# A two-layer convolution block on one core: one xs store a unit, a third place for layer 0's outputs, moved expert and weight steps, Newton square roots

## The chip, the core and the metric

The kernel runs on one core of one Trainium2 chip. The metric is the device time of an execution in microseconds; several executions are made and their median is given. Engines are named as in the profile: PE (matrix multiply), DVE (vector), ACT (scalar, activation), POOL (GpSimd), SP (issues most of the transfers; "SPq" and "ACTq" are the queues of SP and ACT).

## The reference, cut to what matters

The input x has shape (4, 64, 256, 256), float32. Two blocks are added to it in turn, each on a GroupNorm of 32 groups (two channels a group):

```python
x = x + L0(_gn(x))
x = x + L1(_gn(x))

def L0(x):                                   # layer 0
    h = _gelu(_conv2d(x, c1_w, ((1, 1), (1, 1))))          # 3x3, 64 -> 64
    xa, k = jnp.split(_c1x1(h, c2_w, c2_b), 2, axis=1)
    xs = _conv2d(xa, sh_w, ((0, 0), (1, 1)), groups=C) + sh_b   # 1x3, per channel
    xs = _conv2d(xs, sv_w, ((1, 1), (0, 0)), groups=C) + sv_b   # 3x1, per channel
    xs = _gelu(xs)
    weights = softmax(xs.mean(axis=(2, 3)) @ gate_w.T)     # top 2 of 3 kept, in mask
    out = xs
    for i, (w1, b1, w2, b2, w3, b3) in enumerate(experts): # ranks 2, 4, 8
        e = _c1x1(_c1x1(k, w2, b2) * _c1x1(xs, w1, b1), w3, b3)
        out = out + e * mask[:, i][:, None, None, None]
    return _c1x1(out, proj_w, proj_b)

def L1(x):                                   # layer 1
    h = relu(batchnorm(conv3x3(x, quantize(w1), b1)))      # statistics over all images
    h = batchnorm(conv3x3(h, quantize(w2), b2))
    return relu(h + x)
```

## The kernel before, in words

Layer 0 is cut into 64 **units**, 16 an image, each of 16 image rows (8 on each half of the 128 partitions). A unit's 3x3 convolution is made by a transform over rows: POOL forms differences of input rows in a single buffer `v` (`x_fourths`, `x_seconds`, `v_inner`, `v_outer`); PE multiplies them with `us`, the weights scaled by the image's GroupNorm (`front_conv`, tiles `ps_c`, products 1 to 4 first and the outer products 0 and 5 later); DVE puts the products together in PSUM (`butterfly_a` to `butterfly_d`, L631 to L650); ACT takes the GELU (`front_h`, L658). The outer products add onto the bank that `butterfly_c` has just written (L643, L644). The two separable convolutions follow for each half of a unit: PE multiplies the vertical taps (`front_taps_a` and `front_taps_b`, tile `ps_a`, one PSUM place named "a"), ACT and DVE add the horizontal ones (`front_taps_i`, L699; `front_taps_h`, L706 to L717, the last to read the place), and ACT takes the GELU into xs (`front_xs`, L730), whose row sums feed the gate. Between the two tap groups a tick (`divide`, L506, a one-column memset) separates matmuls on the bank; it runs on DVE for the first image and on POOL from slot 16 on.

For every two units PE makes the low-rank parts of the experts: `front_k` (tile `ps_k`, 32 matmuls, from h) in even slots, `front_q` (tile `ps_q`, 16 matmuls, from xs) in odd ones; DVE multiplies the two (`front_low`, L771). xs goes to DRAM with one transfer for each half of a unit, issued by ACT (`xs_store`, L735), the low ranks through SP (`low_store`).

An image's gate needs the mean over all its xs, so its **output** runs an image later: four slots after the image's end, chunk k of the 16 is loaded again (`xs_load` L844, `low_load` L854, and x itself into y, `out_load` L835), PE multiplies with the gated weights (`out_open`, tile `ps_o`), DVE adds onto y (`out_add`, L880) and takes its statistics (L885), SP stores y (`out_store`, L893). The y tiles have the tag "o" with two places. At the same time the GroupNorm statistics of a later image are taken from further loads (`stats_load` L410; `stats_group` on DVE L415, `stats_piece` on ACT L448).

Layer 1 runs over the same images in chunks of 16 rows: `conv1_load` (`yn`), differences on POOL (L343), a split of each operand in an upper and a lower part on ACT and DVE (L346, L353), 128x128 matmuls (L296, tiles `ps_hm` and `ps_h`), and an exit on DVE (`leave`, L318) into h, which ACT squares (L382) and stores (L998). h lies in a place "h1", or, for odd chunks of later images and for odd chunks after the second of the first, in the place "x" that layer 0's loads used (`conv1_out`). Its BatchNorm needs all images; then conv2 runs the same way, and a last pass adds and stores.

**Order of the work.** It is written out by hand. `at(step, order, call)` puts a call in a plan; a unit's slot is two steps, and `at_slot(u, pos, ...)` puts positions below 6 in its first step and 6 to 12 in its second. `plan_front`, `plan_stats`, `plan_out`, `plan_out_late` and `plan_conv1` fill the plan, which is sorted and issued; each engine then runs its own instructions in exactly that order, and a wait of one holds all behind it on that engine. Slots 64 to 66 have no unit of their own, and the table `TAIL` spreads what is left of them over layer 1's steps. "Slot u" below is the time from unit u's first L631 to the next unit's. The order of a slot on PE, which the change touches, is this:

```python
at_slot(u, 2, front_taps_a, u - 2, 1)
at_slot(u, 4, front_taps_b, u - 2, 1)
at_slot(u, 5, front_conv, u, (0, 5))
at_slot(u, 7, front_taps_a, u - 1, 0)
at_slot(u, 8, front_k, ...)   # front_q in odd slots
at_slot(u, 9, front_taps_b, u - 1, 0)
```

**Roots and weights.** `combine` makes a GroupNorm's mean and 1/std out of partial moments: two tiny matmuls with one-column steps between, the square root on ACT (L282), a reciprocal on DVE (L284). It is a generator, advanced at places that the plan names (`stats_end` for the inputs, `out_end` for the outputs). `weights1` quantizes layer 1's two weight sets in three steps each (DVE, L249 to L261), at slots 7 to 12.

Of the kernel before, what the change touches and what calls it, by code (L numbers as in the profile page):

```python
# [11 lines left out]
BF16 = mybir.dt.bfloat16  # L12
AF = mybir.ActivationFunctionType
# [6 lines left out]
P = 128  # L20
# [21 lines left out]
def conv_preact_kernel(ctx: ExitStack, tc: tile.TileContext, io, col128, colset, col64):  # L42
# [82 lines left out]
    eps_bn = const.tile([P, 1], F32, name="eps_bn")  # L125
    nc.vector.memset(eps_bn, BN_EPS)
# [13 lines left out]
    outer = lconst.tile([P, 2, W], F32, name="outer")  # L140
# [33 lines left out]
    def weights():  # L174

        m64_t = work.tile([P, 2, GF], F32, tag="xs", name="m64", bufs=4)
# [22 lines left out]
        for i in range(2):  # L199
            o = outer[:, i, :]  # L200
            nc.vector.tensor_scalar(o, zeros[:, 0:W], sh_bias, None, ALU.add)
            nc.vector.tensor_tensor(o[:, 0 : W : W - 1], o[:, 0 : W : W - 1], end, ALU.subtract)
            nc.vector.tensor_scalar(o, o, c128("sv")[:, 2 * i : 2 * i + 1], None, ALU.mult)
# [41 lines left out]
    def weights1(name):  # L245
# [5 lines left out]
        nc.vector.reciprocal(inv, scale)  # L251
        yield
        nc.vector.tensor_scalar(w, w, inv, ROUND, ALU.mult, ALU.add)
        nc.vector.tensor_scalar(w, w, ROUND, None, ALU.subtract)
        nc.vector.tensor_scalar(w, w, QMAX, -QMAX, ALU.min, ALU.max)
# [7 lines left out]
    def combine(mv, n, avg, eps_t, out, name, engine=nc.vector):  # L263
# [16 lines left out]
        nc.vector.tensor_reduce(var, ps[:, 0:n], AX.X, ALU.add)  # L280
        yield
# [4 lines left out]
    def group_norm(st, avg, out, name, engine):  # L286
        mv = stat.tile([P, 1, 2], F32, tag="mv", name=f"mv_{name}")
        nc.vector.bn_aggr(mv[:, 0, :], flat(st))
        yield
        yield from combine(mv, 1, avg, eps, out, name, engine)  # L290
# [183 lines left out]
    def stats_end(b):  # L474
# [10 lines left out]
        yield from combine(mv, n, c128("avg4"), eps, own, f"x{b}", nc.vector if b == 0 else nc.gpsimd)  # L485
# [215 lines left out]
    def front_taps_h(u, sub):  # L701
# [19 lines left out]
        for at_n, i, row in ((0, 0, 0), (NOCT - 1, 1, 2 * GP - 1)):  # L721
            if n == at_n:
                rows = slice(i * C, i * C + C)
                nc.vector.tensor_tensor(t[rows, row, :], t[rows, row, :], outer[rows, i, :], ALU.subtract)

    def front_xs(u, sub):
        b, k = divmod(u, NCH)
        n = 2 * k + sub
        x = xss[b, n] = work.tile([P, 2, GF], F32, tag="xs", name=f"xs_{b}_{n}", bufs=4)
        nc.scalar.activation(flat(x), flat(open_t.pop((u, sub))), AF.Gelu, accum_out=pooled[b][:, n : n + 1])  # L730

    def xs_store(u, sub):
        b, k = divmod(u, NCH)
        n = 2 * k + sub
        nc.scalar.dma_start(xs_d[b][:, n, :], flat(xss[b, n]))  # L735
# [24 lines left out]
    def front_q(b, j):  # L760
# [874 lines left out]
```

## Time and profile before

| | |
|---|---|
| Median of three executions | 2964.82 us (2963.71 to 2973.92) |
| The profiled execution | 2959.65 us, span 2957.8 us |
| Busy over the span | PE 79%, DVE 83%, ACT 68%, POOL 57% |
| Transfers | 915.35 MB in 135715 packets, 309 GB/s mean |

Times inside the span are counted from its start. The stages, with the limits that the slots and the layers give:

| Stage | from us | to us | length us |
|---|---|---|---|
| Statistics of image 0, slots 0 and 1 | 0 | 98.0 | 98.0 |
| Slots 2 to 11, image 0, no output yet | 98.0 | 278.0 | 180.0 |
| Slots 12 to 19 | 278.0 | 422.9 | 144.9 |
| Slots 20 to 24, output of image 0 begins | 422.9 | 516.2 | 93.3 |
| Slots 25 to 43 | 516.2 | 899.0 | 382.8 |
| Slots 44 to 62 | 899.0 | 1258.5 | 359.5 |
| Start of layer 1 | 1258.5 | 1331.5 | 73.0 |
| Rest of conv1 | 1331.5 | 1923.0 | 591.5 |
| conv2 | 1923.0 | 2514.0 | 591.0 |
| Last pass | 2514.0 | 2957.8 | 443.8 |

How to read the views. A table of stretches gives the busy microseconds of each engine in each stretch (with the number of instructions), the granted clock of PE as a share, the mean busy share of the 16 DMA engines, and GB/s. A chain of waits is followed back from the last instruction of a window, each time to what released it: start, length, engine and what it did; "issue" is time without a wait that the trace shows. A row of waits names who waited for whom, with the sum in us, the count and the longest. Names like `ps_a` or `y` are tiles; "a<-b" is written from b.

### The profile page before, as it was taken

Reading aid. Unit: us, or ns where it says so; the run is one execution under the profiler, and the core shown is the slowest. Engines: PE = TensorE matmul, PEld = TensorE weight load, DVE = VectorE, ACT = ScalarE, POOL = GpSimd, SP = SyncE. Lnnn points to the kernel's source line nnn. Section 1 sums busy time; section 2 is a strip of 40 time slices with the busy share of each in tenths; the row PEclk is TensorE's granted clock in tenths of the full one; section 3 lists DMA queues with packets and bytes.
Section 4 is the critical chain, followed back from the end, with each engine's and each line's share of the span. In section 5 each row is a group of like instructions: output and inputs, shape, how many; then the busy total and the mean of one; then the engine's idle time right before and its main releaser. Section 6 shows DMA issues by size and latency. Waiting matters only on the chain.

```text
span 2957.8 us, 52737 instructions
## 1 busy us (share of the span) xinstructions
PE 2345.4 (79%) x21576; PEld 1502.1 (51%) x21576; DVE 2448.4 (83%) x2811; ACT 2007.1 (68%) x2183; POOL 1676.8 (57%) x1252
## 2 busy tenths in 40 slices
PE   2888899999999999979999999989999999000000
PEld 1444445444445555546666667867788888000000
DVE  6688678888888988869999999979999898976664
ACT  4777888787776665567676667978888887432221
POOL 6988888787778888733545546735555555000000
PEclk9999999999999999999999999999999999555555
DMA  8665579999999999859999997747777764999999
GB/s 352 233 239 209 199 269 369 354 351 350 355 349 320 320 319 327 290 203 320 343 367 361 332 360 272 270 176 274 258 267 264 270 219 156 375 412 423 420 424 409
DMA packets 135715, 915.35 MB, mean 309 GB/s; under 512 B 14960, under 2 KB 15728, under 8 KB 40880
## 3 DMA queue, kind: packets, MB, share of 16 engines
q1 hardware_dynamic: 107824, 777.74, 71.1%
q10 hardware_dynamic: 27648, 134.23, 11.3%
q8 instruction: 170, 2.79, 0.4%
q14 instruction: 73, 0.60, 0.1%
HBM read 573.74 MB, written 338.17 MB: 308 GB/s over the span
## 4 chain that ended last, share of the span: by engine, by line
PE 50%; DMA 29%; DVE 13%; ACT 3%; POOL 2%; issue 2%; SPq 0%; ACTq 0%; DVEq 0%; POOLq 0%
PE ps_h L296 18%; PE ps_c L513 9%; DMA y<-in_xp 7%; PE ps_a L513 7%; PE ps_h2m L296 6%; DMA y_end<-y_d 5%; DMA y_d<-y 4%; DMA out<-h 4%; DMA h<-h_d 4%; PE ps_o L513 4%; DMA yn<-y_d 3%; PE ps_hm L296 3%; DVE t L714 2%; DVE t L717 2%; PE ps_k L744 1%
## 5 line engine op out<-in xcount | busy, mean ns | idle before, releaser
L296 PE MATMUL ps_h<-diff,w_q 128*128 128x512 f32 x3072 | 755.2, 400 | 12.4 <-DVE h L318 11.9
L296 PEld LDWEIGHTS ps_h<-diff,w_q 128*128 128x128 f32 x3072 | 577.0, 189 | 190.6 <-issue 20.4
L513 PE MATMUL ps_c<-v,us 64*64 64x256 f32 x9216 | 534.0, 380 | 28.6 <-DVE ps_c L644 25.4
L343 POOL TENSOR_TENSOR d<-yn 128x1024 f32<-128x1024 f32 x128 | 348.9, 2745 | 299.3 <-DMA yn<-y_d 164.8
L513 PEld LDWEIGHTS ps_c<-v,us 64*64 64x64 f32 x9216 | 360.7, 134 | 174.4 <-issue 17.6
L343 POOL TENSOR_TENSOR d<-h 128x1024 f32<-128x1024 f32 x126 | 307.1, 2459 | 206.4 <-DVE diff L351 143.6
L513 PE MATMUL ps_a<-h,av 64*64 64x512 f32 x4080 | 386.5, 492 | 47.3 <-DVE t L717 40.1
L318 DVE SCALAR_TENSOR_TENSOR h<-ps_h,scale_w,m 128x1024 f32<-128x1024 f32 x256 | 323.1, 1279 | 78.7 <-PE ps_h L296 56.3
L561 POOL TENSOR_TENSOR x<-x 128x512 f32<-128x512 f32 x256 | 328.8, 1284 | 12.7
L1497 ACT ACTIVATE h<-h,shift,gn 128x2048 f32<-128x2048 f32 (+1 forms) x65 | 134.3, 2067 | 276.0 <-DVE h L1496 273.8
L513 PEld LDWEIGHTS ps_a<-h,av 64*64 64x64 f32 x4080 | 153.7, 133 | 322.2 <-issue 212.8
L382 ACT ACTIVATE junk<-h,less_h 128x2048 bf16<-128x2048 f32 (+3 forms) x134 | 256.2, 1912 | 13.6 <-DVE h L318 13.5
L1496 DVE SCALAR_TENSOR_TENSOR h<-h,inverse,y_end 128x2048 f32<-128x2048 f32 (+1 forms) x65 | 150.5, 2317 | 122.0 <-DMA y_end<-y_d 122.0
L699 ACT ACTIVATE t<-ps_a,tap_bias,m 128x1016 f32<-128x1016 f32 x128 | 153.3, 1197 | 117.0 <-PE ps_a L513 91.4
L880 DVE SCALAR_TENSOR_TENSOR y<-ps_o,ob,y 128x1024 f32<-128x1024 f32 x128 | 164.0, 1281 | 50.9 <-PE ps_o L513 26.6
L730 ACT ACTIVATE xs<-t 128x1024 f32<-128x1024 f32 x128 | 134.8, 1053 | 103.8 <-DVE t L717 90.2
L353 DVE SCALAR_TENSOR_TENSOR diff<-d,gn,diff 128x1024 fp32r<-128x1024 f32 x128 | 202.0, 1608 | 0.9 <-ACT diff L346 0.5
L296 PE MATMUL ps_h2m<-odd,w_q 128*128 128x512 f32 x768 | 193.5, 401 | 5.9 <-ACT odd L359 3.8
L296 PE MATMUL ps_hm<-odd,w_q 128*128 128x512 f32 x768 | 194.0, 402 | 2.8 <-DVE t L717 1.3
L346 ACT ACTIVATE diff<-d 128x1024 fp32r<-128x1024 f32 x128 | 135.3, 1057 | 81.1 <-POOL d L343 79.5
L553 POOL TENSOR_TENSOR x<-x,x 128x512 f32<-128x512 f32 x128 | 160.5, 1275 | 34.2 <-ACT x L547 34.2
L717 DVE SCALAR_TENSOR_TENSOR t<-ps_a,m,t 128x1020 f32<-128x1020 f32 x128 | 163.9, 1280 | 4.6
(256 smaller groups left out, 4235.2 us busy)
## 6 DMA issues: line engine op xcount, KB each, us to landing
x<-in_xc SPq DMA_DIRECT2D x64, 1280.0 KB
h<-h_d SPq DMA_DIRECT2D x64, 1152.0 KB
yn<-y_d SPq DMA_DIRECT2D x60, 1152.0 KB
xs_in<-in_xp SPq DMA_DIRECT2D x64, 1024.0 KB
xs_d<-xs ACTq DMA_DIRECT2D x128, 512.0 KB
xs_in<-xs_d SPq DMA_DIRECT2D x64, 1024.0 KB
y<-in_xp SPq DMA_DIRECT2D x64, 1024.0 KB
y_d<-y SPq DMA_DIRECT2D x64, 1024.0 KB
```

What stands on the lines that cost most here:

```text
L296: nc.tensor.matmul(ps, wq[w][:, kind, kx, :], t[:, rows, kx : kx + W], start=(j == 0), stop=(j == len(terms) - 1))
L318: nc.vector.scalar_tensor_tensor(h.rearrange("p (e k) w -> p e (k w)", e=2), ps.rearrange("p e k w -> p e (k w)"), w_scale[w], m.unsqueeze ...
L343: engine.tensor_tensor(raw.rearrange("p (g r) w -> p g r w", g=2), *pair, ALU.subtract)
L353: nc.vector.scalar_tensor_tensor(lower, raw, scale, upper.bitcast(F32), ALU.mult, ALU.subtract)
L382: nc.scalar.activation(junk[rows, 0:n], flat(h), AF.Square, bias=less[name][rows], accum_out=total)
L513: last[:] = [nc.tensor.matmul(ps[o, at_out[0] : at_out[1], :], w[i], rhs[i], **flags)]
L553: nc.gpsimd.tensor_tensor(x4[:, j - 1], x_rows(u, j + 2), x4[:, j - 1], ALU.subtract)
L561: nc.gpsimd.tensor_tensor(x[:, r : r + 2], x[:, r + 2 : r + 4], x[:, r : r + 2], ALU.subtract)
L699: nc.scalar.activation(t[:, :, inside], ps[:, :, inside], AF.Identity, bias=tap_bias, scale=sh[:, 1:2])
L717: nc.vector.scalar_tensor_tensor(t[:, :, 0 : W - 1], ps[:, :, 1:W], sh[:, 2:3], t[:, :, 0 : W - 1], ALU.mult, ALU.add)
L880: nc.vector.scalar_tensor_tensor(y, ps.rearrange("p x s w -> p x (s w)"), out_bias[b], y, ALU.add, ALU.add)
L1496: nc.vector.scalar_tensor_tensor(at_h, at_h, inverse[:, b : b + 1], y[:, a:e, :], ALU.mult, ALU.add)
```

## The change

Layer 0's xs gets one tile for both halves of a unit (two of them, where there were four half tiles), stored with one transfer at the place of the second half's. The y tiles get a third place in layer 0's own pool for every third chunk. In slots up to 19, `front_k` stands at position 4.5 instead of 8, and so does `front_q` for three of its four half units, with the fourth left at 8. The DVE statistics at position 4.1 go to 6.125 in slots below 16. `weights1` has four steps, at slots 5 to 8 and 9, 10, 11 and 14. The square roots of the GroupNorms other than the first go to three Newton steps on POOL from a bit estimate on DVE; BatchNorm's stay on ACT. In layer 1, h of chunk 1 of image 0 lies in the place "x", the row differences of both halves share a tile, the second splits of chunk 1 stand behind the taps, and y of the late outputs is stored a step later. `outer` keeps one row a partition, and the second epsilon column goes.

The diff, cut:

```diff
+    HALF = 0.5
+    MAGIC = 1597463007.0
+    def root(var, n, y, name):
+        nc.vector.tensor_scalar(var, var, 1.0 / n, eps, ALU.mult, ALU.add)
+        nc.vector.tensor_scalar(y.bitcast(I32), var.bitcast(I32), -HALF, MAGIC, ALU.mult, ALU.add)
+        t = stat.tile([P, 1], F32, tag="ct", name=f"root_{name}")
+        for _ in range(3):
+            yield
+            nc.gpsimd.tensor_scalar(t, var, y, y, ALU.mult, ALU.mult)
+            nc.gpsimd.tensor_scalar(t, t, -HALF, 1.0 + HALF, ALU.mult, ALU.add)
+            nc.gpsimd.tensor_tensor(y, y, t, ALU.mult)
...
         nc.vector.tensor_reduce(var, ps[:, 0:n], AX.X, ALU.add)
+        if step:
+            yield from root(var, n, out[:, 1:2], name)
+            return
...
     def front_xs(u, sub):
-        x = xss[b, n] = work.tile([P, 2, GF], F32, tag="xs", name=f"xs_{b}_{n}", bufs=4)
-        nc.scalar.activation(flat(x), flat(open_t.pop((u, sub))), AF.Gelu, accum_out=pooled[b][:, n : n + 1])
+        if sub == 0:
+            xss[u] = work.tile([P, 2, 2, GF], F32, tag="xs", name=f"xs_{u}", bufs=2)
+        x = xss[u][:, sub].rearrange("p s f -> p (s f)")
+        nc.scalar.activation(x, flat(open_t.pop((u, sub))), AF.Gelu, accum_out=pooled[b][:, n : n + 1])
-    def xs_store(u, sub):
-        nc.scalar.dma_start(xs_d[b][:, n, :], flat(xss[b, n]))
+    def xs_store(u):
+        nc.scalar.dma_start(xs_d[b][:, 2 * k : 2 * k + 2, :].rearrange("p a b -> p (a b)"), x)
...
     def out_load(b, k):
-        ys[b, k] = chunk_out(f"y_{b}_{k}", "o", 2)
+        if k % 3 == 2 and (b < B - 2 or b == B - 2 and k < 11):
+            ys[b, k] = front_pool.tile([P, CPAIR, W], F32, tag="third", name=f"y_{b}_{k}")
+        else:
+            ys[b, k] = chunk_out(f"y_{b}_{k}", "o", 2)
...
     def conv1_out(b, k, g):
-            if k % 2 and (b > 0 or k > 2):
+            if k % 2:
...
-                at_slot(u, 6.135, xs_store, u - 2, 1)
+                at_slot(u, 6.135, xs_store, u - 2)
-                at_slot(u + 1, 1.6, xs_store, u - 1, 0)
+            alone = u < NCH + 4
-                at_slot(u, 8, front_k, *divmod(j, NOCT // 4))
+                at_slot(u, 4.5 if alone else 8, front_k, *divmod(j, NOCT // 4))
-                at_slot(u, 8, front_q, *divmod(j, NOCT // 4))
+                if alone:
+                    at_slot(u, 4.5, front_q, *divmod(j, NOCT // 4), range(3))
+                at_slot(u, 8, front_q, *divmod(j, NOCT // 4), range(3 if alone else 0, 4))
...
-            for n in range(3):
-                at_slot(7 + 3 * i + n, 7.3, next, chain, None)
+            for u in ((5, 6, 7, 8), (9, 10, 11, 14))[i]:
+                at_slot(u, 7.3, next, chain, None)
...
-                at_slot(int(s), 4.1 if s - int(s) < 0.5 else 7.25, stats_group, b, *group)
+                early = 6.125 if int(s) < NCH else 4.1
+                at_slot(int(s), early if s - int(s) < 0.5 else 7.25, stats_group, b, *group)
...
-                at(step + 1, 13.3, out_store, b, n // 2)
+                at(step + 2, 13.3, out_store, b, n // 2)
...
-            at(*late(up0, 13.12), conv1_upper, b, k, 0)
-            at(*late(up1, 13.14), conv1_upper, b, k, 1)
+            behind = b == 0 and k == 1
+            at(*late(up0, 13.36 if behind else 13.12), conv1_upper, b, k, 0)
+            at(*late(up1, 13.37 if behind else 13.14), conv1_upper, b, k, 1)
-            at(*((t, 1.3) if first else late(low0, 13.22)), conv1_lower, b, k, 0)
+            at(*((t, 1.3) if first else late(low0, 13.45 if behind else 13.22)), conv1_lower, b, k, 0)
```

## The prediction

> **What bounds the kernel now.** I cut the span into stages, with slot borders at the starts of L631 (the first butterfly instruction, one a slot), and read the busy time of each engine in each.[...]
>
> ```profile
> 98.00:203.60 105.60, 93.00 (x1381) 50.80 (x1375) 82.17 (x124) 84.04 (x117) 92.41 (x73) 1.00 0.67 232
> 203.60:278.00 74.40, 63.99 (x952) 34.62 (x944) 63.00 (x93) 53.20 (x72) 64.69 (x50) 1.00 0.56 200
> ...
> 422.90:516.20 93.30, 93.16 (x1336) 48.19 (x1329) 81.55 (x104) 76.32 (x108) 76.68 (x71) 1.00 1.00 372
> 516.20:899.00 382.80, 359.42 (x5033) 183.70 (x5028) 317.69 (x414) 299.27 (x420) 298.16 (x296) 1.00 0.96 350
> 899.00:1258.50 359.50, 358.79 (x5060) 185.79 (x5056) 317.57 (x410) 217.55 (x268) 293.78 (x295) 1.00 0.91 315
> 1258.50:1331.50 73.00, 53.78 (x382) 30.61 (x371) 47.23 (x55) 43.22 (x48) 26.84 (x17) 0.94 0.55 204
> ```
>
> The columns: stretch, length, busy us of PE, weight loads, DVE, ACT, POOL, granted clock, DMA share, GB/s. Slots 44 to 62 (899 to 1258.5) are PE without a gap, and so are slots 20 to 24. Time above PE's busy time is lost in three places: slots 2 to 19, slots 25 to 43 (23.4 us), and the start of layer 1 (19.2 us). I asked each for its chain of waits. In slots 2 to 19 no engine is full:
>
> ```profile
> 154.80 0.69 DVE ps_c L644
> 155.49 1.19 DVE st_x L415 x2
> 156.68 0.14 DVE t L706
> 156.82 0.02 issue
> 156.85 1.29 DVE t L714
> 158.14 0.02 issue
> 158.16 1.29 DVE t L717
> 159.45 0.14 issue
> 159.59 2.38 PE ps_a L513 x24
> 161.97 1.85 PE ps_q L766 x16
> 163.82 0.59 PE ps_a L513 x8
> 164.42 5.24 PE ps_c L513 x94
> ```
>
> Two statistics instructions stand ahead of the taps, whose last instruction (L717) frees the one "a" bank; only then does PE go on, and k or q stand in the rest of its path. In slots 25 to 43:
>
> ```profile
> 589.49 13.76 DMA y_d<-y
> ...
> 603.33 20.72 DMA y<-in_xp
> 624.05 0.04 DVEq L880
> ```
>
> A store of y frees a place, the load into it lands, the next sum and store follow at 629.40: 39.9 us for two slots, since there are two places. That is the stage's pace: 382.8/19 = 20.15 a slot against PE's 18.92. At the start of layer 1:
>
> ```profile
> DVE h L318 <- DMA h_d<-h: 12.5, 1, 12.5
> PE ps_h L296 <- DVE h L318: 8.6, 1, 8.6
> ```
>
> Chunks 1 and 2 of h share the one "h1" place; chunk 2 waits for chunk 1's store, and PE behind it.
>
> **k and q of image 0, and the statistics (slots 2 to 19).** Nothing is added: k's 32 matmuls, and 12 of q's 16, move ahead of the outer products. In slot 6 of the timeline PE stood 0.23 us for the tick, 0.77 for L644 ahead of the outer products and 0.72 for L717 (1.13 in slot 7). With 1.9 us of k or q put into the 0.77, and 1.2 us of statistics behind the taps, L717 is through before PE needs the bank: 17.38 - 0.77 - 0.72 and 17.76 - 0.77 - 1.13, plus 0.23 in each for a tick now uncovered behind the taps, gives 16.1 a slot. ACT, behind a statistics piece and k's copy, reaches its first copy up to 0.8 us later than PE would, so I take 16.3. The moved statistics now stand ahead of DVE's second tick; with the butterfly before them they are 2.7 us beside a tap group of 2.38 on PE, which itself starts later, so they hide, or cost 0.3. Slots 2 to 7: 105.6 to 98.2, -7.4. Bounds: 15.5 (PE's 93.00/6), and 17.6, no gain, should POOL (92.41/6 = 15.4, ahead of its waits) set the pace.
>
> Slots 8 to 11 lose more: slots 8 and 11 took 19.29 and 20.50, each with three weight instructions in a row (1.18 + 1.52 + 1.05 us) ahead of the taps. The change lays one to a slot; at most the copies (2.1 us) stand together. I take 16.6 a slot with what spills over: 74.4 to 66.4, -8.0. Slots 12 to 15 took 73.4 with PE at 63.5 and ACT at 63.4: 68.1, -5.3. In 16 to 19 the tick is POOL's, in order behind the row differences. k used to stand between the two tap groups and hid that tick; moved, it pushes the outer products and the POOL work waiting on them by about as much as it saves. I take 0, bounds -4 and +4. Together -21.
>
> **Newton steps.** Seven of eight GroupNorm roots leave ACT. L282's table loads read 1283 ns; the square root itself 0.29 us, and the gelu table comes back: 2 x 1.28 + 0.29 = 2.9 us of ACT each. The Trainium skill ("ScalarE: Activation LUTs", What ACT_TABLE_LOAD costs) adds a drain of about 1.38 us per switch, so 5.6; the group's idle time ahead of its seven loads here is 0.1 us in all, so I use 2.9. It is worth something only in slot 14 (ACT 17.9 of 19.29, counted above); elsewhere ACT has 3 us of slack a slot. Added: two DVE instructions near 0.2 for a reciprocal, and nine POOL ones per root near 0.19 (the gate's L814) with their issue, 2.4 us in three places, behind which row differences queue. POOL has 3 us of slack a slot where PE is full. In layer 1 DVE's last product waits for POOL's third step, with its lower differences (L353) and exits (L318) queued behind: before it waited for ACT's root, so -1 to +4 in all; I take +1.
>
> **Third place for y (slots 25 to 43).** The loop of 39.9 us now spans three slots, 13.3 each: gone. Next late is PE at 359.4 us, or the transfers: the stage moved 134.17 MB. Here a rule speaks against the change. The Trainium skill ("DMA: Bandwidth & Descriptors", Where 436 GB/s comes from) has HBM bind a core at about 358 GB/s. By it the stage can't be under 134.17/0.358 = 374.8 us, a gain of 8. But slots 20 to 24, the same streams before the loop binds, ran 372 GB/s with PE full, and the end reaches 424 in the page's last slices. The row decides: 134.17/0.370 = 362.6, -20. Bounds -8 and -23.4 (PE).
>
> **One xs store a unit.** 64 transfers of 1 MB for 128 of half: ACT issues 64 fewer (0.33 us of its queue each, beside its work), and the same bytes move. By the trace's packets 4 KB on ACT's queue take 159 ns at the median, 8 KB in layer 1 309: 2.8% of a seventh of the traffic, under 0.1 us a slot, which the 370 leaves out. Some ACT issues also wait for a y store (six ACT waits, 17.6 us); those go with SP's lag. The new wait is in the rivals.
>
> **Start of layer 1.** h of chunk 1 goes to the x place, so chunk 2 needs chunk 0's store, issued at 1303.91; with the same 11.4 us it lands at 1315, before ACT's m is through at 1319.8. DVE then starts near 1319.9 instead of 1330.17, and PE, done with its last group at 1322.95, loses its 8.57 us. Chunk 1's differences now stand behind the taps; PE waited 3.35 us at 1281 for L717, behind a L353 that waited for ACT: -2. If k's buffer or POOL's differences (wait of 12.6 for q) are late instead, half is left. -10, bounds -5 and -13.
>
> The stores of y one step later in layer 1 and the smaller edge tile pass nothing on SP's queue that a wait depends on, and the weights' first tile is loaded once: 0.
>
> **Sum.** -21 - 20 - 10 + 1 = -50: 2909.6 on the profiled execution, 2914.8 on the median. I say 2914.
>
> **Rivals.**
> - HBM binds as the rule has it: 8 instead of 20, so 2926. For it: share 0.96 to 1.00 already. Against: 372 in slots 20 to 24. 0.17.
> - POOL takes over in slots 2 to 15: of 21 only the weights' 5 remain, 2930. For it: 15.4 us of work and waits on PE and ACT in each slot. Against: those waits (2 us a slot) are behind PE, which gets earlier. 0.13.
> - Everything lands at its floor: slots 2 to 15 near 15.9 (-26) and 25 to 43 at PE's 359.4, the start at -13: 2903. 0.14.
> - Slower: the unit's xs tile comes free only when one 1 MB store, issued behind both halves, has landed. From the second half's store to the GELU that takes the place again: 610.9 to 640.6, 29.7 us. Half stores there end 7.4 to 9.0 us after issue by their packets, so I estimate 13 for 1 MB. Above 29.7 ACT stops in order, with h and the taps behind it; at 50/43 = 1.2 us a slot over that (a store of 31 us) the gains are eaten, beyond it the kernel is slower: at 33 us, 43 x 2.1 more, 3005. 0.06.
>
> **How the numbers follow.** The sum as worked out has 0.50. The range 2895 to 2938 reaches over the first three rivals with the bounds of the stages, and leaves out the slow case and double misses. A change of 0.5% (15 us) is what a measurement of this kernel can tell from none. Faster takes the first four cases but for double misses: 0.88; same 0.06; slower 0.06.
>
> **What would show it.** In the stage from slot 25 to 43: no wait of SP's y load for a y store, DMA at 365 to 380 GB/s, PE busy 97% or more; if PE is short of that at a share of 1.00, the first rival. In slots 2 to 7: L717 no longer ends PE's wait, slots near 16.3; if POOL's busy share passes 97%, the second. Slots 8 and 11 no longer stand out. At the start of layer 1: no L318 waiting for h_d, PE's gap of 8.57 gone. ACT's GELU (L730) waiting for the xs store would make it wrong. Layer 1 after its start (591.5 us), the second convolution (591.0) and the end (443.8) should keep their times within 5 us each.

## The result and the profile after

The changed kernel takes 2952.14 us (median of six runs, 2947.45 to 2959.98) against 2973.6 for the kernel before on the same chip. The ratio of the two means is 0.9938, 95% interval [0.9916, 0.996], so it is 0.6% faster, where 1.7% was forecast. Its profiled execution took 2947.45 us with a span of 2945.6, so between the two profiled executions 12.2 us of span are to be placed. Cut at the same borders:

| Stage | before | after | difference | forecast |
|---|---|---|---|---|
| to slot 2 | 98.0 | 97.1 | -0.9 | 0 |
| slots 2 to 7 | 105.6 | 99.7 | -5.9 | -7.4 |
| slots 8 to 11 | 74.4 | 68.4 | -6.0 | -8.0 |
| slots 12 to 19 | 144.9 | 143.4 | -1.5 | -5.3 |
| slots 20 to 24 | 93.3 | 95.5 | +2.2 | 0 |
| slots 25 to 43 | 382.8 | 383.7 | +0.9 | -20 |
| slots 44 to 62 | 359.5 | 360.8 | +1.3 | 0 |
| slot 63 to chunk 4 of layer 1 | 81.0 | 67.6 | -13.4 | -10 |
| chunks 4 to 16 | 135.8 | 149.0 | +13.2 | 0 (Newton +1) |
| chunks 16 to 48 | 350.8 | 345.6 | -5.2 | 0 |
| all after that | 1131.7 | 1134.8 | +3.1 | 0 |

Chunk borders are PE's first matmul of a chunk. The means differ by 18 us and the profiled spans by 12.2, because the profiled execution of the kernel before (2959.65 us) is quicker than all six timed ones. Its slots 25 to 43 took 382.8 us; three further kernels that have the uneven load described below and two places of y took 389.2 (e3), 390.8 (e7) and 392.0 (e8) there. The changed kernel repeats better: 383.7, and 383.3 and 383.9 in e5 and e6.

The stages that matter, in the table of stretches of the kernel after (length, busy of PE, weight loads, DVE, ACT, POOL, granted clock, DMA share, GB/s):

```profile
97.10:196.80 99.70, 96.97 (x1379) 50.04 (x1373) 84.89 (x127) 83.98 (x117) 91.57 (x73) 1.00 0.67 241
196.80:265.20 68.40, 66.30 (x948) 34.85 (x941) 58.53 (x91) 52.07 (x71) 61.81 (x49) 1.00 0.59 225
...
504.10:887.80 383.70, 360.52 (x5035) 184.34 (x5028) 318.87 (x416) 294.25 (x414) 302.38 (x314) 1.00 0.93 348
887.80:1248.60 360.80, 358.81 (x5060) 184.60 (x5056) 318.02 (x412) 211.88 (x262) 297.60 (x313) 1.00 0.90 315
1248.60:1310.00 61.40, 52.95 (x381) 30.60 (x374) 47.27 (x56) 39.57 (x45) 23.54 (x17) 0.97 0.51 189
```

Slots 2 to 11 did shrink, and PE is 97% busy there. The start of layer 1 (last line) is some 61 us, where it was 73.0. Slots 25 to 43 kept the length of the profiled execution before: PE still loses 23 us, now with the DMA engines busy for 0.93 and not full. In slots 2 to 7 the waits of PE itself were, before, for the last of the taps (L717) and for L644. After, the only one of any length is for the tick, and L736, now the last of the taps, is not among them. The first two lines are from before:

```profile
PE ps_a L513 <- DVE t L717: 6.4, 6, 1.1
PE ps_c L513 <- DVE ps_c L644: 4.7, 6, 0.9
...
PE ps_a L532 <- DVE tick_v L525: 2.6, 9, 0.6
```

The waits in slots 25 to 43 after, first of the computing engines, then of SP's queue; the last line of each fence is from before:

```profile
DVE y L906 <- DMA y<-in_xp: 28.7, 9, 4.5
...
PE ps_o L532 <- DVE y L906: 11.6, 8, 2.1
...
DVE y L880 <- DMA y<-in_xp: 16.1, 9, 3.5
```

```profile
SPq L919 <- DVE y L906: 103.1, 19, 11.1
...
SPq L861 <- DMA y_d<-y: 8.3, 1, 8.3
...
SPq L835 <- DMA y_d<-y: 82.5, 19, 7.7
```

(L906 adds onto y, L861 loads y, L919 stores it.) The second fence shows that the third place did what it was made for: SP's load of y waits for a store of y once, 8.3 us, where before it did so 19 times for 82.5 us. The first shows what stands in its place: DVE waits for the loads themselves, 28.7 us where it was 16.1, and PE waits for DVE behind it. Why is a load late that was issued in time? The timeline of the kernel after, SP's queue and the sum on DVE:

```profile
782.19 2.48 SPq L880 DMA_DIRECT2D ranks<-low_d  x2
784.76 1.19 SPq L870 DMA_DIRECT2D xs_in<-xs_d  x1
787.30 0.39 SPq L429 DMA_DIRECT2D xs_in<-in_xp  x1
790.96 0.33 SPq L861 DMA_DIRECT2D y<-in_xp  x1
...
815.21 1.28 DVE L906 SCALAR_TENSOR_TENSOR y<-ps_o,ob,y 128x1024 f32<-128x1024 f32 x1 [4.25 <-DMA y<-in_xp]
```

The load of y is issued at 790.96, and the sum that needs it starts at 815.21, 24 us later. A transfer is split in shares, one for each DMA engine that it uses, and the trace records each landing of a share (a step of the transfer's semaphore). For this one:

```text
y<-in_xp issued 790.96: twelve shares at 798.4 to 801.6, then 808.8, 812.1, 814.7, 815.1
ranks<-low_d issued 782.19: one step at 783.4, then four shares at 794.6, 798.5, 800.8, 802.1
```

Twelve shares are there within 10.7 us of the issue. Four come 7 to 13.5 us after those. And the two loads of the low ranks that SP issued before it (`low_load`, 256 KB each) have only four shares, apart from one step right after the issue (1.2 and 2.0 us): they run on four of the 16 DMA engines. Their packets are of 4 KB with a median of 159 ns; 512 KB on four engines are 32 packets each, 5.1 us of work every second slot that the other twelve engines don't have. What is queued behind on these four lands late, and a transfer is ready when its last share is.

This is so for all of the stage, not for one load. Read from the landings in the traces, medians over slots 25 to 43, us:

| | before | after | e1 | e2 | e9 | f |
|---|---|---|---|---|---|---|
| y load: last share behind the twelfth | 9.8 | 12.5 | 1.3 | 1.3 | 1.3 | 1.3 |
| y load: issue to last share | 16.2 | 21.4 | 13.1 | 15.2 | 13.9 | 12.7 |
| y store: issue to last share | 15.0 | 15.3 | 5.0 | 5.1 | 13.9 | 7.3 |
| xs store (ACT's queue): last share behind the twelfth | 1.3 | 1.3 | 1.1 | 1.0 | 1.2 | 1.1 |

(e1, e2, e9 and f are the runs below in which the low ranks come in 16 shares.) The tail of four shares stands in the y loads and stores of SP's queue. The xs stores, which use ACT's queue, have none even with the uneven load: what is late is what stands behind the low ranks in the same queue.

The Trainium skill ("DMA: Bandwidth & Descriptors", Why a DMA increments its semaphore by 16 and not by 1) has this as a rule: the number of engines is the largest up to 16 that divides the slowest dimension of both sides. The load's DRAM side is written with an outer dimension of 4 (`(i x r) f -> x i r f`), the tile's with 64; that gives 4, as the trace has it.

### The profile page after: what moved, and what is told of

Read it like the earlier page. It is cut to its first block, busy times and chain, and to the rows that moved or that the text cites. A ratio compares the mean times of both kernels' runs of the same rounds, so it can differ in the third digit from the quotient of the medians.

```text
span 2945.6 us, 52716 instructions
## 1 busy us (share of the span) xinstructions
PE 2355.8 (80%) x21576; PEld 1499.0 (51%) x21576; DVE 2450.1 (83%) x2817; ACT 1992.6 (68%) x2166; POOL 1675.7 (57%) x1315
## 4 chain that ended last, share of the span: by engine, by line
PE 27%; DMA 20%; DVE 5%; POOL 2%; issue 1%; ACT 1%; SPq 0%; ACTq 0%; DVEq 0%; POOLq 0%
PE ps_h L315 17%; PE ps_h2m L315 6%; DMA y_end<-y_d 5%; DMA out<-h 4%; DMA h<-h_d 4%; DMA yn<-y_d 4%; PE ps_hm L315 3%; DMA xs_in<-xs_d 2%; POOL d L362 1%; DVE diff L372 1%; DVE h L337 1%; PE ps_o L532 1%; DMA y<-in_xp 1%; DVE h L1525 1%; DVE h L1533 1%
## 5 line engine op out<-in xcount | busy, mean ns | idle before, releaser
L362 POOL TENSOR_TENSOR d<-yn 128x1024 f32<-128x1024 f32 x128 | 330.2, 2602 | 296.4 <-DVE diff L372 141.4
L532 PEld LDWEIGHTS ps_c<-v,us 64*64 64x64 f32 x9216 | 358.2, 134 | 170.8 <-issue 17.2
L532 PE MATMUL ps_a<-h,av 64*64 64x512 f32 x4080 | 383.8, 489 | 27.9 <-DVE t L736 12.7
L337 DVE SCALAR_TENSOR_TENSOR h<-ps_h,scale_w,m 128x1024 f32<-128x1024 f32 x256 | 322.9, 1279 | 60.7 <-PE ps_h L315 49.9
L401 ACT ACTIVATE junk<-h,less_h 128x2048 bf16<-128x2048 f32 (+3 forms) x134 | 256.3, 1913 | 13.6 <-DVE h L337 13.5
L718 ACT ACTIVATE t<-ps_a,tap_bias,m 128x1016 f32<-128x1016 f32 x128 | 153.4, 1199 | 107.1 <-PE ps_a L532 103.8
L906 DVE SCALAR_TENSOR_TENSOR y<-ps_o,ob,y 128x1024 f32<-128x1024 f32 x128 | 164.0, 1281 | 71.8 <-DMA y<-in_xp 32.4
L751 ACT ACTIVATE xs<-t 128x1024 f32<-128x1024 f32 x128 | 134.8, 1053 | 117.5 <-DVE t L736 105.3
L372 DVE SCALAR_TENSOR_TENSOR diff<-d,gn,diff 128x1024 fp32r<-128x1024 f32 x128 | 203.3, 1619 | 0.0
L315 PEld LDWEIGHTS ps_h2m<-odd,w_q 128*128 128x128 f32 x768 | 146.3, 191 | 42.6 <-ACT odd L378 3.9
```

Source lines behind the costliest of these rows:

```text
L315: nc.tensor.matmul(ps, wq[w][:, kind, kx, :], t[:, rows, kx : kx + W], start=(j == 0), stop=(j == len(terms) - 1))
L337: nc.vector.scalar_tensor_tensor(h.rearrange("p (e k) w -> p e (k w)", e=2), ps.rearrange("p e k w -> p e (k w)"), w_scale[w], m.unsqueeze ...
L362: engine.tensor_tensor(raw.rearrange("p (g r) w -> p g r w", g=2), *pair, ALU.subtract)
L372: nc.vector.scalar_tensor_tensor(lower, raw, scale, upper.bitcast(F32), ALU.mult, ALU.subtract)
L401: nc.scalar.activation(junk[rows, 0:n], flat(h), AF.Square, bias=less[name][rows], accum_out=total)
L532: last[:] = [nc.tensor.matmul(ps[o, at_out[0] : at_out[1], :], w[i], rhs[i], **flags)]
```

## The experiments

All kernels were compared with the kernel before on their own chip; times are medians, ratios are of means and have a 95% interval. Stages are those of the table. "The rows load" means the loads of the low ranks.

| Label | from | time us | ratio |
|---|---|---|---|
| e1_rows_after | after | 2915.22 | 0.9838 [0.9803, 0.9873] |
| e2_rows_before | before | 2930.2 | 0.9878 [0.9851, 0.9905] |
| e3_two_places | after | 2959.6 | 0.9971 [0.996, 0.9982] |
| e4_low_twice | after | 3262.98 | 1.0997 [1.0956, 1.1037] |
| e5_act_roots | after | 2951.45 | 0.992 [0.9894, 0.9947] |
| e6_store_step | after | 2958.12 | 0.9953 [0.993, 0.9975] |
| e8_h_place | before | 2965.13 | 0.9978 [0.9959, 0.9996] |
| e9_low_by_16 | after | 2917.02 | 0.9816 [0.9789, 0.9844] |
| e7_front | before | 2960.4 | 0.9974 [0.9956, 0.9991] |
| f_before16 | before | 2936.04 | 0.9898 [0.9876, 0.9919] |
| g_even_act | e9 | 2916.08 | 0.9828 [0.9808, 0.9847] |
| h_even_two | e9 | 2921.39 | 0.9841 [0.9814, 0.9868] |
| i_q_whole | e9 | 2922.08 | 0.9836 [0.9813, 0.986] |
| j_kq_back | e9 | 2926.67 | 0.985 [0.9825, 0.9876] |

**The rows load in one run of 64 rows.** The same bytes in transfers of the same size; only the outer dimension of 4 goes. The rows land in another order, so the experts' part of the output is not the reference's in these two.

```diff
-            low = low_d[b][:, k // 2, :].rearrange("(i x r) f -> x i r f", i=4, x=2)
+            low = low_d[b][:, k // 2, :].rearrange("(x p) f -> x p f", x=2)
```

On the changed kernel:

> The changed kernel, but the two loads of the low ranks for a pair of chunks read rows 64x to 64x+63 of the stored ranks in one run of rows instead of four runs of 16 (so wrong ranks reach the output; bytes, packets and number of transfers are the same). Theory A: each of these loads, 256 KB, runs on four of the sixteen DMA engines, because its outer dimension is 4; these four carry some 2.5 us a slot where the others carry none of it, and they set the pace of slots 25 to 43. Then the stage of 383.7 us falls to PE's 361 to 366 and the time by 15 to 22 us against the changed kernel (2925 to 2937 if that is at 2947 to 2952). Theory B, the sum of the traffic (7 MB a slot at 350 to 370 GB/s) sets the pace: nothing changes, within 3 us. Theory C, SP's queue in order (the y store waits for DVE, everything behind it): nothing changes either, within 5 us.

On the kernel before:

> The kernel before with the same single edit (runs of 64 rows, wrong ranks in the output). Theory A: y's load and store land when the slowest of their sixteen engines does, so the loop of store and load over two places, 39.9 us, is itself lengthened by the four loaded engines; with even engines both land 5 to 10 us sooner, the loop falls under PE's 37.8 and the stage of 382.8 us falls to 362 to 368: 2945 to 2955 against 2965 to 2973 before. Then the third place was not needed. If two places bind on their own (the prediction's theory), the stage stays within 5 us of 382.8.

Slots 25 to 43 in the stretches of e1:

```profile
502.80:865.90 363.10, 358.23 (x5032) 184.26 (x5028) 320.19 (x415) 294.03 (x414) 302.87 (x314) 1.00 0.96 367
```

And of e2:

```profile
514.70:879.70 365.00, 358.66 (x5032) 186.03 (x5028) 319.68 (x414) 299.32 (x420) 298.77 (x296) 1.00 0.97 366
```

They come within 4.9 and 6.3 us of PE's own busy time. The second is the kernel before with its two places of y: the loop of 39.9 us per two slots, on which the prediction built, goes with the form of a load, and no third place is needed for it. SP's wait for a y store falls from 82.5 us to this:

```profile
SPq L835 <- DMA y_d<-y: 6.7, 8, 1.3
```

By the table of landings most of the loop's excess was the store's last four shares (15.0 us from issue to the last, 5.1 here); the load's own time falls by 1.0. The times fell further than was expected, since the even load shortens chunks 4 to 48 of layer 1 too: 149.0 and 345.6 us after, 144.2 and 340.0 in e1; in e2 chunks 16 to 48 take 337.1, 350.8 before.

**The rows load twice.**

```diff
                 nc.sync.dma_start(at_low, low[x])
+                nc.sync.dma_start(at_low, low[x])
```

> The changed kernel with each load of the low ranks issued twice, the second over the first with the same data: 0.26 MB a slot more, 3.7% of the traffic. Theory A: the four engines get 2.5 us a slot more, so slots 25 to 43 grow by 35 to 55 us, and slots 44 to 62, so far at PE's pace, by 0 to 30 as well. Theory B: slots 25 to 43 grow by about 14 us (3.7%), slots 44 to 62 not at all. Theory C: by the issue of one to two transfers, under 5 us in all.

The stage takes 482.3 us, 98.6 more, 5.2 a slot for 256 KB a slot more, some 4% of the traffic. That is about twice what theory A expected, and slots 44 to 62, which were at PE's pace, take 433.7 for 360.8: the direction is A's, the size is not. In this kernel stretches occur in which only these loads run; the stretches of 547 to 549, where other transfers run, and of 551 to 552 and 553 to 556:

```profile
547.00:549.00 2.00, 2.00 (x32) 0.94 (x28) 1.52 (x2) 1.89 (x3) 1.69 (x2) 1.00 0.94 373
551.00:552.00 1.00, 1.00 (x25) 0.69 (x20) 0.96 (x2) 0.92 (x2) 0.99 (x2) 1.00 0.25 98
553.00:556.00 3.00, 2.74 (x36) 1.06 (x28) 2.90 (x6) 2.62 (x5) 0.95 (x3) 1.00 0.25 94
```

The last two columns are the point: a share of 0.25 is 4 engines of 16, and they move 94 to 98 GB/s, a quarter of the 373 above. So the four engines are shown here by a second view. Why the doubling costs 5.2 us a slot, when its packets make only 2.5 of work on each of the four, is not settled. SP also stood in its queue for it: one of these issues starts at 546.97 and the next at 557.26.

**The rows load in transfers of 16 rows.** Each outer index becomes a transfer of its own (64 KB).

```diff
-                at_low = flat(lows[b, k // 2])[64 * x : 64 * x + 64, :]
-                nc.sync.dma_start(at_low, low[x])
+                for i in range(4):
+                    at_low = flat(lows[b, k // 2])[64 * x + 16 * i : 64 * x + 16 * i + 16, :]
+                    nc.sync.dma_start(at_low, low[x, i])
```

On the changed kernel:

> The changed kernel with right ranks over all engines: each load of 64 rows is four transfers of 16 rows, so that the outer dimension is 16. Theory A: slots 25 to 43 fall from 383.7 to 362 to 368 and the time to 2915 to 2925, as with the rows in one run. Against it stands the price of six more transfers every two slots: SP's queue and the eight semaphores that transfers take in turn in the trace; if these bind, the stage stays at 372 to 390.

```profile
505.00:869.90 364.90, 358.39 (x5033) 185.29 (x5028) 319.50 (x415) 293.96 (x414) 302.45 (x314) 1.00 0.95 366
```

The line is e9's stretch of slots 25 to 43. DVE's wait for the load of y falls from 28.7 us to 6.3 in six waits. By the medians it is 35 us faster than the changed kernel, and it beats both kernels. On the kernel before:

> The kernel before, with each 64-row load of the low ranks split into four transfers of 16 rows, nothing else. If the four overloaded DMA engines make the loop of y's two places, slots 25 to 43 fall from 382.8 to about 365 us with two places, and the kernel lands near 2928, ratio 0.987, like the one-run form of the same load. Rival: SP's queue, which now issues six more transfers per pair of chunks, holds the y loads up: the stage stays above 375 and the ratio is over 0.993.

Its stage takes 368.9 and the whole 2936.04: of the 17.9 us that e9 gains in slots 25 to 43 on the profiled execution before, this edit alone gives 13.9, and the one run of 64 rows (e2) 17.8.

**The third place, taken away.** First on the changed kernel, then on e9:

```diff
-        if k % 3 == 2 and (b < B - 2 or b == B - 2 and k < 11):
+        if False:
```

> The changed kernel without the third place: all y tiles in the two places again. Theory A: slots 25 to 43 stay within 5 us of 383.7, the third place moves no more than a wait; the time within 5 us of the changed kernel. The prediction's theory, that the two places bind and only then something else: the same or up to 5 us slower. If the third place did give something that was lost elsewhere, 10 to 20 us slower.

> The changed kernel with the loads of the low ranks split into 16 rows, but without the third place for layer 0's outputs. If the third place is worth next to nothing once the DMA engines are loaded evenly, slots 25 to 43 stay within 2 us of the 364.9 with three places, and the time within 3 us of 2917. Rival: with the tail of the transfers gone the two places become the limit of their own, 368 to 372 in that stage and 2921 to 2925.

With the uneven load, four executions with two places took 382.8 (before), 389.2 (e3), 390.8 (e7) and 392.0 us (e8) in this stage, and three with the third place 383.7, 383.3 (e5) and 383.9 (e6). So the third place is worth some 5 us of the stage on the mean, though nothing against the one profiled execution before; by the times it is worth 0.3%, with intervals that touch. With the even load: 366.0 without, 364.9 (and 366.1 in g) with it. There it is worth about 1 us in its own stage, and the times (2921.39 without, 2917.02 with) have ratios whose intervals overlap.

**The front's moves alone, on the kernel before.** k, q and the statistics of image 0 moved, and the weights in four steps:

```diff
-                at_slot(u, 8, front_k, *divmod(j, NOCT // 4))
+                at_slot(u, 4.5 if alone else 8, front_k, *divmod(j, NOCT // 4))
...
+                if alone:
+                    at_slot(u, 4.5, front_q, *divmod(j, NOCT // 4), range(3))
+                at_slot(u, 8, front_q, *divmod(j, NOCT // 4), range(3 if alone else 0, 4))
...
+            for u in ((5, 6, 7, 8), (9, 10, 11, 14))[i]:
+                at_slot(u, 7.3, next, chain, None)
...
+                early = 6.125 if int(s) < NCH else 4.1
```

> The kernel before with only the front's moves for image 0 (k and q ahead of the outer products, the statistics group behind the taps, the weights of layer 1 in four steps spread over the slots). If the moves are what shortens slots 2 to 19, the stages of slots 2 to 7 and 8 to 11 measure 100 and 68 us as in the changed kernel and slots 12 to 19 about 144, 12 to 13 less in all; the stage of slots 25 to 43 keeps 383 and the start of layer 1 its 81. About 2952 to 2960, ratio 0.995. Rival: part of the 13 us comes from the single xs store or the Newton roots: then slots 2 to 19 give under 8, and the ratio is over 0.997.

Slots 2 to 11 take 168.2, as in the changed kernel (168.1), so the xs store and the roots have no part in that gain. Slots 12 to 19 take 147.0 for 143.4 after and 144.9 before: slot 14, where the first root of another image ran on ACT, stays at 19.29 here and fell to 17.04 in the changed kernel, and slot 19 took 18.54 for 17.21, as it also did once in e9. The whole gained 0.26%; the interval, 3 to 13 us, holds the 9.6 us of these stages. The profiled execution, the longest of this kernel's, took 390.8 us in slots 25 to 43, but that is not the moves' doing: e8, whose edit touches layer 1 alone, took 392.0 there.

**q in one piece again; then k and q both back.** On e9:

```diff
-                if alone:
-                    at_slot(u, 4.5, front_q, *divmod(j, NOCT // 4), range(3))
-                at_slot(u, 8, front_q, *divmod(j, NOCT // 4), range(3 if alone else 0, 4))
+                at_slot(u, 8, front_q, *divmod(j, NOCT // 4))
```

The second kernel has instead `alone = False`. The reason for these two was found in the timeline of PE in slot 7 of the kernel after:

```profile
183.48 1.92 PE L789 MATMUL ps_q<-xs,m 128*32 128x512 f32 x12
185.32 2.82 PE L532 MATMUL ps_c<-v,us 64*64 64x256 f32 x48
187.97 2.33 PE L532 MATMUL ps_a<-h,av 64*64 64x512 f32 x24
190.23 1.90 PE L789 MATMUL ps_q<-xs,m 128*32 128x512 f32 x4
```

Slot 7 before has one piece:

```profile
197.04 1.92 PE L766 MATMUL ps_q<-xs,m 128*32 128x512 f32 x16
```

Twelve of q's matmuls take 1.92 us and the four left behind take 1.90: each fills 32 of the 128 output rows, the four half units run side by side, and the four of one half unit alone last as long as sixteen together. Over slots 2 to 19 ps_q is busy for 34.4 us where it was 17.6, with 144 matmuls in both.

> The changed kernel with the low ranks loaded in 16 rows, and q of image 0 in one piece again, behind the taps as before; k stays moved. Theory: q's split into 12 and 4 matmuls costs TensorE a second 1.9 us in each of nine slots (ps_q busy 17.6 us before, 34.4 after, for the same 144 matmuls), and that is what slots 2 to 19 fall short of the forecast by. Then ps_q falls back to 17.6 us, and as the odd slots get back their 0.77 us ahead of the outer products and a wait for the taps of about 0.7, they gain about 0.4 to 1.1 us each: slots 2 to 19 from 311 to 302 to 308, the kernel 3 to 9 under 2917. Rival: the odd slots are held by DVE, ACT or the ticks, the split lies in cover, and slots 2 to 19 stay at 311 or grow.

> The same, with k and q of image 0 both at their places of before (the statistics, the weights, the xs store and the roots stay changed). If moving k earns the gain of the even slots (17.4 to 15.4 and 16.6), they return to about 17 and slots 2 to 19 to some 316 to 322, slower than the kernel with q whole by 10 or more. Rival: the statistics behind the taps and the spread weights earn the gain; then slots 2 to 19 stay below 312.

The theory fell. With q whole, ps_q is back at 17.6 us, but slots 2 to 19 take 313.1 us, where the kernels with the split take 311.5 (after, e5, g and h; 313.0 in e9, whose slot 19 took 18.53). The odd slots stay where they were or grow (slot 7: 17.32 for 17.25). What they wait for changed. Slot 7 after, and slot 7 with q whole, in the table of stretches:

```profile
179.60:196.80 17.20, 16.68 (x220) 8.17 (x216) 15.45 (x23) 15.09 (x23) 16.01 (x14) 1.00 0.57 215
...
180.60:198.00 17.40, 15.33 (x224) 8.51 (x220) 15.96 (x23) 15.26 (x23) 17.00 (x15) 1.00 0.57 217
```

PE loses 1.35 us of work and gets it back as gaps, which its timeline with q whole names:

```profile
185.56 2.83 PE L532 MATMUL ps_c<-v,us 64*64 64x256 f32 x48 [0.86 <-DVE ps_c L663]
189.06 2.38 PE L532 MATMUL ps_a<-h,av 64*64 64x512 f32 x24 [0.68 <-DVE t L736]
```

L663 is `butterfly_c`, L736 the last of the taps: the two waits that the move was made to fill are back. Followed back from two slots later, the chain of waits with the split runs through PE alone from the tick at 182.8 to the end of slot 7, with both pieces of q in it. With q whole it runs from the tick through the taps on ACT and DVE (L718 to L736, 184.8 to 188.9) to PE. POOL stands on neither, though it is busy for 17.00 of 17.40 us. So the split trades a second 1.9 us of q for the wait for the one bank "a", and the two cost nearly the same. With k back too, slots 2 to 19 take 318.0, and every slot from 5 to 10 some 17.4. Of the 13.4 us that these slots gain in all, the statistics with the weights and the root in slot 14 are worth 6.9, k's move 4.9 and q's split 1.6.

**The start of layer 1: h of chunk 1 in the other place, alone, on the kernel before.**

```diff
-            if k % 2 and (b > 0 or k > 2):
+            if k % 2:
```

> The kernel before with one part of the change: h of chunk 1 of layer 1 in the place x. The stretch from slot 63 to chunk 4 of conv1 falls from 81.0 to 69 to 73. If what follows is set by PE, all of it is kept: 8 to 11 us off 2965 to 2973. If what follows is set by transfers that start when layer 0 ends (yn, y, the ranks on four engines), chunks 4 to 16 take 5 to 10 us longer than 135.8 and 0 to 5 us are kept.

The wait of L318 for h_d is gone here and after, and with it PE's gap of 8.57 us. In e8 the start takes 72.3 for 81.0, and chunks 4 to 16 then 142.6 for 135.8: of 8.7 us, 6.8 are given back at once. The changed kernel gains 13.4 and gives back 13.2. Three runs ask what takes it. First, the roots of layer 0's outputs back on ACT, on the changed kernel and on e9:

```diff
-        yield from combine(mv, 1, avg, eps, out, name, engine, True)
+        yield from combine(mv, 1, avg, eps, out, name, engine)
...
-                (e + 3, 5.6), (e + 3, 7.4), (e + 4, 2.45)):
+                (e + 3, 4.45), (e + 3, 8.3)):
```

> The changed kernel with the roots of the four output GroupNorms on ACT again, at their old places; the Newton steps of the three input ones stay. Of the start of layer 1's 13 us of gain, all is gone again between chunks 4 and 16 of conv1 (149.0 us against 135.8). Theory N: 5 to 6 of it is DVE's product behind POOL's third Newton step (DVE waited 5.6 us there, POOL being held up by its row differences); then chunks 4 to 16 fall to 141 to 145 and the time by 4 to 8. Theory Y: the loop of the late y tiles over two places takes it; then chunks 4 to 16 stay within 2 us of 149.0 and so does the time.

> The changed kernel with the loads of the low ranks split into 16 rows, and the roots of layer 0's second GroupNorm back on ACT at their places of before. If Newton's roots on POOL cost 2 to 3 us in chunks 4 to 16 of layer 1, as the run with the roots back on ACT alone showed (146.3 for 149.0), that stage falls from 143.4 to about 141 and the kernel to about 2914, ratio 0.981. Rival: the roots only wait where DVE is full anyway, and the stage stays at 143 to 144, 2917.

Then the store of y at its step of before:

```diff
-                at(step + 2, 13.3, out_store, b, n // 2)
+                at(step + 1, 13.3, out_store, b, n // 2)
```

> The changed kernel with the late y stores one step earlier, as before. Theory Y: each late y load waits for the store of two chunks before it (SP waits 40.7 us for this in chunks 4 to 16), and a step of 2.5 us between them is 2.5 us of that loop: chunks 4 to 16 fall by 4 to 9 us. Theory N, or if SP waits for DVE longer than the step anyway: within 2 us of 149.0, and the time within 3 us of the changed kernel.

Chunks 4 to 16 take 146.3 in e5, 148.6 in e6, 143.4 in e9 and 143.4 in g (149.0 after). The roots' 2.7 us of e5 do not come back once the rows load is even, so it can't be said that they cost anything; the store's step costs nothing in this stage either. In chunks 16 to 48, where late y stores run as well, it does seem to count: three kernels with the later store and the uneven load take 345.6 to 347.8 us there (after, e3, e5), and four without it 350.8 to 356.7 (before, e6, e7, e8). Of these e6 differs from the kernel after by the store alone: 356.7 for 345.6, one profile each. With the even load it is worth nothing: 337.1 in f without it, 339.6 in e9 with it.

The even load is worth 5.6 us of chunks 4 to 16. What holds the rest is mostly DVE, by the chain of waits: through these chunks it is 75% PE in f, where h lies as before, and in e9 47% DVE and 19% PE. Chunks 4 to 16 of e9, in the table of stretches, and its chain in the middle of them:

```profile
1297.20:1440.60 143.40, 132.17 (x654) 89.31 (x653) 134.16 (x153) 96.56 (x93) 72.09 (x36) 0.99 0.91 347
```

```profile
1366.38 2.49 DVE h L337 x4
1368.87 1.14 DVE odd L381
1370.01 3.34 DVE diff L372
1373.35 1.21 DVE y L907
...
1375.20 0.55 DVE st_y L912
1375.79 1.27 DVE diff L372
1377.06 2.41 DVE h L337 x4
1379.47 1.14 DVE odd L381
1380.60 3.35 DVE diff L372
```

DVE is busy for 134.16 of 143.4 us, PE for 132.17, and the chain goes from one DVE instruction to the next: exits of h (L337), lower parts (L372, L381), and the sums of the last image's output (L907). Before, the same chunks had 127.20 of DVE in 135.7. DVE did not get that much more to do: the same instructions take longer. The row of one kind of them, the lower parts, in f and in e9:

```profile
L353 DVE SCALAR_TENSOR_TENSOR diff<-d,gn,diff 128x1024 fp32r<-128x1024 f32 x24 | 32.6, 1362 | 0.0
...
L372 DVE SCALAR_TENSOR_TENSOR diff<-d,gn,diff 128x1024 fp32r<-128x1024 f32 x25 | 44.6, 1788 | 0.0
```

In the chain above one of them takes 1.27 us and two take 3.3. In the traces of before, f, e8, after and e9, those beside which POOL did nothing took 1.28 us at most. Those of over 3 us (4, 1, 5, 7 and 6 of 24) each ran beside one of POOL's row differences for two thirds of their time or more. So begun earlier, this work of DVE meets POOL's more often, in a stage in which DVE has next to no time left. That is read from the traces; no run takes work from DVE or moves POOL's.

## Why the prediction was wrong

By its own steps, in the order of their size.

**The third place for y: -20 forecast, +0.9 measured (-5 against the mean of four executions with two places). This is the step that failed**, in the sentence "Next late is PE at 359.4 us, or the transfers". The loop did go, as the waits show. But "the transfers" was worked out as a sum of bytes over a rate, 134.17 MB at 370 GB/s, as if all 16 engines carried the same. Four of them carried 5.1 us more in every second slot, and these four set when a load of y is whole. The same four had made the loop of 39.9 us itself, so a third place took away a symptom. The mean DMA share of 0.96, which the prediction weighed only as a sign of HBM, does not show that four shares of a y load landed 10 to 12 us behind the other twelve. With the load even, the stage takes 364.9, near the forecast's 362.6, with 366 GB/s: the HBM rule's floor of 374.8 us, which the prediction weighed and set aside, did not bind, and the first rival falls with it.

**The start of layer 1: -10 forecast, -0.2 kept.** The mechanism was right and the start gave more than forecast (-13.4), but the step asked only for what is next in the start and not for the stage behind: there DVE was 94% busy (127.20 of 135.7), its instructions got longer beside POOL's, and 13.2 were given back. Of this the uneven load holds 5.6; e9 keeps 7.0 of the two stages' 216.8. That the rest is DVE is read from the chain and not tested.

**Slots 2 to 19: -21 forecast, -13.4 measured.** Slots 2 to 11 gave 11.9 of 15.4. "Nothing is added" was wrong, since q's 16 matmuls in two pieces cost PE their 1.9 us twice. That holds most odd slots at 17.2 to 17.4, and putting it right gains nothing, because the wait for the taps comes back. The even slots fell to 15.2 to 16.7, where 16.3 to 16.6 was forecast for all. The second rival, POOL taking over, did not come: its share in slots 2 to 7 is 91.57 of 99.70, under the 97% that was set as its sign, and it stands on neither chain of slot 7. In slots 12 to 15 the forecast of 68.1 had no sum behind it. Slot 14 fell by 2.25 with the root, but slot 15 grew from 18.67 to 19.82; with k and q back it is 18.14, and the four slots take 71.6 for 71.5, so the moves earn nothing there.

**Right:** the Newton steps' +1 (no more than the intervals, by g against e9); the xs store at nothing, with no wait of ACT's GELU (L751) for it, so the slower rival didn't come (its 1 MB lands 8.9 us after the issue, the median of slots 25 to 43, where 13 was estimated); the taps no longer ending PE's waits in slots 2 to 7; the end of the wait for h_d. The slower rival has a slip in its sum: 43 x 2.1 us stand over the time at which the gains are eaten, so 33 us would have given some 3055 and not 3005. **Not forecast:** -5.2 in chunks 16 to 48, where the prediction put the later store at 0; e6 makes that store its likely source. The even load gives more there: -11.2 in e9, and -13.7 in e2, which has the even load alone.

The forecast time was reached only by taking away the cause that it had not seen: e9 with 2917.02 us. The change's own part of that is 19 us by the medians, or 24 by the ratios, over the kernel before with the same even load (2936.04); the rest is the load's.

## What to carry to other kernels

Before a transfer-bound stage is costed by bytes over a rate, count the shares of each transfer: here one load whose outer dimension is 4 put its bytes on four engines, and what stood behind it in the same queue waited for those. A loop of "store, then load, then compute" that is longer than its transfers' own time should be asked why each landing is late before it is given another buffer. Time that is freed ahead of a stage with a nearly full engine may be given back there. And a stage should be seen in several executions before 5 us of it are explained: the same code of one stage took 382.8 to 392.0.

## What the runs showed of the hardware

A load of 256 KB with an outer dimension of 4 ran on 4 of 16 DMA engines, at 94 to 98 GB/s and a share of 0.25; four loads of 16 rows of 4 KB in its place took the whole kernel from 2952.14 to 2917.02 us, and on the kernel before from 2966.91 to 2936.04. In the y loads of slots 25 to 43 the last four shares landed 9.8 (before) and 12.5 us (after) behind the twelfth, and 1.3 with the even load; the xs stores on ACT's queue had 1.3 with the uneven load too. Four matmuls of 32 output rows took 1.90 us where sixteen, on four such quarters side by side, took 1.92. A DVE instruction on 128x1024 elements (L353 before, L372 after) took up to 1.28 us with POOL idle, and over 3 beside one of POOL's row differences.
